# Moving a sort's transposes between matmul steps, and reordering the seven products of one Strassen job

## Chip, cores and metric

The kernel runs on one core of a Trainium2 chip. The metric is the device time of one execution in microseconds. The whole network is one launch; all arithmetic is float32 (a few indices are int32).

Engine names in the profile: PE is TensorE's matmuls and PEld its weight loads, DVE is VectorE, ACT is ScalarE, POOL is GpSimd, SP is SyncE, which only issues DMAs here.

## What is computed

An image of 1024 channels by 64 x 64 pixels goes through four residual layers, each after a group norm:

```python
x = x + _L0_conv_ref(_gn(x), ...)   # per-pixel decay scan over the channels
x = x + _L1_conv_ref(_gn(x), ...)   # 1x1 convolution, 1024 -> 1024
x = x + _L2_conv_ref(_gn(x), ...)   # in_proj, conv, scan in permuted order, gate, out_proj
x = x + _L3_conv_ref(_gn(x), ...)   # 1x1 convolution
```

In layer 2 the pieces that matter here are:

```python
xz = silu(in_proj_w @ x + in_proj_b)
x_ssm, res, gate = split(xz, 3)
xf = silu(conv1d(x_ssm, dw_w) + dw_b)          # three taps along the tokens
perm = _mobius_perm(mobius, H, W)              # per head: argsort of 4096 scores
dbc = dbc_w @ xf + dbc_b                       # dt, B, C of the scan
y = scan(gather(xf, perm), gather(dbc, perm))  # then scattered back
y = y * silu(gate) + res
x = x + silu(out_proj_w @ y + out_proj_b)
```

## The kernel before

The image is kept as 8 blocks of 512 tokens (`FB`), and two blocks make a pair, so there are four pairs (`NP`). All large matrix products use the Strassen-Winograd form: seven products P1 to P7 of half-sized blocks replace eight, at the price of sums on the other engines. With A the weights and B the activations, the outputs are C11 = P1 + P2, C12 = P1 + P6 + P5 + P3, C21 = P1 + P6 + P7 + P4 and C22 = P1 + P6 + P7 + P5 (signs are in the operands).

**The stage with the sort.** The argsort is a bitonic sort of both heads' 4096 scores, written as a generator, `sort_work` (L287). Its `compare` (L295) is eleven small VectorE instructions. For the last five of its twelve rounds the keys have to be transposed and transposed back, which `turn_over` (L324) does: two TensorE transposes into a PSUM bank from `ps_tp`, then a ScalarE copy out of it. The pool behind `ps_tp` has two banks under the tag "tp". The generator yields a word ahead of each piece of work, "compare" or "turn", and `sort_on(quiet, n)` (L373) runs the generator on by at most n compares and returns at each "turn". The sort is a background job: the loops over the matmul steps call `sort_on` once a step with an allowance of compares. Rounds up to 9 are done in layer 1's loop (L915). The rest is done in the loop of L1117, which computes the x_ssm part of in_proj: 56 steps of one product each, 14 a pair, two halves a step. `run(..., fine=True, tell=True)` (L829) yields True in the middle of a product, False after it, and None once the fills of the next pair's operands are issued.

In the same loop the finished tokens go through the convolution and are turned into rows: `follow` (L1040) takes the sums that are ready through `conv`, two steps later into `due3`, and `turn` (L989) does eight matmuls (named l2pt) through two "tp" banks for each of two 128-channel pieces, copies them out on ScalarE to l2xt, adds a part of them on GpSimd, and stores the rest to `tok_d`. The first piece of `due3` is turned in the middle of a step, the other in `follow`.

When the sort is done, its order is stored to `perm_d` and read back as gather indices `src` and scatter indices `dst_` (L361 to L369), all DMAs on GpSimd's queue. The scan stage after it gathers rows by `src`.

On VectorE, TensorE, GpSimd and ScalarE the order of issue in these stages is the program's (`manual_schedule`).

**The two-level jobs.** The gate and out_proj products and layer 3 run in `two_steps` (L1303), with Strassen-Winograd on two levels, 49 products a job, one job a pair and matrix. A job's time is counted in slots, one product each; `plan` (L1376) writes the work of the other engines into a table by slot, `at`. Outer product s of a job has its inner products P1, P2, P6, P7 in slots 7s, 7s+2, 7s+4, 7s+6 and P5, P4, P3 in slots 7s+8, 7s+10, 7s+12, interleaved with the next outer product. Each inner product reads a sum of B's blocks, made by `inner_sum` on GpSimd (four a step), and `emit` (L1492) adds each result into five SBUF tiles: Z (P1, then P6), D (P3), C (P2 + Z), V (P7 + Z, then P4) and Q (P5). At the end C is C11, D is C12, V is C21, Q is C22. For an out_proj job the outer order is `ORDER_B`, P1, P3, P2, P6, P7, P5, P4. `add_in` (L1413) makes the sums between tiles: Z += Q, Q += V, D += Z, a quarter at a time.

The last out_proj job is `final`: its tiles go at once through Silu (ScalarE), the residual sum and `bn_stats` (VectorE) in the slots of the table `done`. After its last statistic comes the group norm of layer 3 (`norm3`, L1552), which the next `two_steps` waits for.

Of the kernel before, what the change touches and what calls it, by code (L numbers as in the profile page):

```python
# [13 lines left out]
ALU = mybir.AluOpType  # L14
# [39 lines left out]
         "P4": (2, "t4"), "P3": (6, "b22")}  # L54
ORDER_A = ["P1", "P2", "P6", "P7", "P5", "P4", "P3"]
ORDER_B = ["P1", "P3", "P2", "P6", "P7", "P5", "P4"]


HN = N // 2
# [29 lines left out]
def tile_net(ctx: ExitStack, tc: tile.TileContext, x, par_d, cst_d, w_d, w2_d, dbcw_d, out):  # L89
    nc = tc.nc  # L90
# [196 lines left out]
    def sort_work():  # L287

        eng, bits = nc.vector, 7
        flip = cst[: HEADS * NT, CST["flip"]]

        def compare(t, new, bit):  # L295
            def two(x):
                v = x.rearrange("p (u s l) -> p u s l", s=2, l=2 ** bit)
                return v[:, :, 0], v[:, :, 1]

            rows, _, w = t.shape  # L300
            a, b = two(t.rearrange("p c w -> p (c w)"))
            (ka, kb), (ia, ib) = two(t[:, 0]), two(t[:, 1])
            (ka2, kb2), (ia2, ib2) = two(new[:, 0]), two(new[:, 1])
            over = swap[0][:rows, :, : w // 2]
            same = swap[1][:rows, 0, : w // 2]
            step = swap[1][:rows, 1, : w // 2]
            def like(x):
                return x.rearrange("p (u l) -> p u l", l=2 ** bit)
            for i, (x, y) in enumerate(((ka, kb), (ia, ib))):
                eng.tensor_tensor(like(over[:, i]), x, y, ALU.is_gt)  # L310
            eng.tensor_tensor(like(same), ka, kb, ALU.is_equal)
            eng.tensor_tensor(same, same, over[:, 1], ALU.mult)
            eng.tensor_tensor(ka2, ka, kb, ALU.min)
            eng.tensor_tensor(same, same, over[:, 0], ALU.add)
            eng.tensor_tensor(like(step), ib, ia, ALU.subtract)
            eng.tensor_tensor(kb2, ka, kb, ALU.max)
            eng.tensor_tensor(step, step, same, ALU.mult)
            eng.tensor_tensor(ia2, ia, like(step), ALU.add)
            eng.tensor_tensor(ib2, ib, like(step), ALU.subtract)

        def negate(v):
            eng.tensor_scalar(v, v, -1.0, None, ALU.mult)

        def turn_over(t, new):  # L324
            rows, _, w = t.shape
            yield "turn"
            pt = ps_tp("sort")
            for c in range(2):
                nc.tensor.transpose(pt[:w, c * rows : (c + 1) * rows], t[:, c], ident[:rows, :rows])
            yield "turn"  # L330
            nc.scalar.copy(new.rearrange("p c w -> p (c w)"), pt[:w, : 2 * rows])  # L331

        now, other = lines
        negate(now.rearrange("p c (u s l) -> p (c u) s l", s=2, l=2)[:, :, 1])
        for k in range(1, 13):
            if k > bits:
                t, t2 = turned_
                yield from turn_over(now, t)
                for bit in reversed(range(k - bits)):
                    yield "compare"  # L340
                    compare(t, t2, bit)
                    t, t2 = t2, t
                yield from turn_over(t, now)
            for bit in reversed(range(min(k, bits))):
                yield "compare"
                compare(now, other, bit)
                now, other = other, now
            if k + 1 < bits:
                v = now.rearrange("p c (u t s l) -> p (c u) t s l", t=2, s=2, l=2 ** k)
                negate(v[:, :, 0, 1])  # L350
                negate(v[:, :, 1, 0])
            elif k + 1 == bits:
                v = now.rearrange("p c (s l) -> p c s l", s=2)
                for s in range(2):
                    eng.tensor_scalar(v[:, :, s], v[:, :, s], flip[:, s : s + 1], None, ALU.mult)
            elif k < 12:
                i = k - bits + 2
                eng.tensor_scalar(now, now, flip[:, i : i + 1], None, ALU.mult)
        eng.tensor_copy(order_i, now[:, 1])
        yield "turn"  # L360
        nc.gpsimd.dma_start(perm_d.rearrange("(a p) o -> a (p o)", p=P), order_i)  # L361
        yield "turn"
        for h in range(HEADS):
            r0, full = h * LC + S, (NK - 1) * LT
            perm = perm_d[h * N : (h + 1) * N]
            for idx in (src, dst_):
                nc.gpsimd.dma_start(idx[r0 : r0 + LT, : NK - 1],
                                  perm[:full].rearrange("(k r) o -> r (k o)", r=LT))
                nc.gpsimd.dma_start(idx[r0 : r0 + N - full, NK - 1 :], perm[full:])  # L369

    coming = [None]

    def sort_on(quiet, n):  # L373


        while coming[0] is not None:
            was = coming[0]
            if was == "compare":
                if n == 0 or not quiet:
                    return  # L380
                n -= 1
            coming[0] = next(order, None)
            if "turn" in (was, coming[0]):
                return


# [566 lines left out]
    with tc.tile_pool(name="l2a", bufs=2) as pa, tc.tile_pool(name="l2a2", bufs=1) as pa2, \  # L953
# [158 lines left out]
        with tc.manual_schedule(engines={E_.DVE, E_.PE, E_.Pool, E_.Activation}):  # L1112
# [4 lines left out]
            for half in run(EARLY + LATE, [WX], normed(norm2), put2a, add2a, before2,  # L1117
                            last_eng=nc.vector, fine=True, tell=True):
                if half:
                    if due3:  # L1120
                        turn(*due3.pop(0))
                elif half is False:
                    follow()
                if half is not None:
                    continue
                i += 1
                if i > 14 and i % 14 == 4:
                    ends = finish(i // 14 - 1)
                next(ends, None)
                sort_on(True, (0, 0, 0, 1, 3, 1, 0, 2, 0, 2, 3, 3, 0, 0)[i % 14])  # L1130
            while coming[0] is not None:
                sort_on(True, 1)

# [158 lines left out]

    wq = ctx.enter_context(tc.tile_pool(name="wq", bufs=10, reuse_waits="tile"))
    xq = ctx.enter_context(tc.tile_pool(name="xq", bufs=4, reuse_waits="tile"))
    bq = ctx.enter_context(tc.tile_pool(name="bq", bufs=13, reuse_waits="tile"))
# [4 lines left out]

    def two_steps(jobs, norm, src_d):  # L1303

        at = {}
        held = {}
        inner = {}
# [68 lines left out]
        def plan(j):  # L1376
            kind, m, pair = jobs[j]
            s0 = j * JOB
            final = j == len(jobs) - 1
            order = ORDER_B if kind == "out" else ORDER_A  # L1380

            def on(slot, f, *a):
                then(s0 + slot, lambda: f(*a))
# [11 lines left out]
            else:  # L1395
                late = [(14, "t1", "b12", "b11"), (15, "t2", "b22", "t1"), (19, "t3", "t2", "b11"), (34, "t4", "b21", "t2")]
                ks = [(2, 3, 0, 1), (2, 3, 0, 1), range(KH), range(KH)]
                put_in = {1: 4, 3: 19}
            for (slot, to, a, b), kk in zip(late, ks):
                for i, k in enumerate(kk):  # L1400
                    on(slot + i, comb, j, to, a, b, k)

            def alias(to, old):
                held[j, to] = tile_of(j, old)
            at[s0 + late[0][0]].insert(0, lambda: alias("t1", "b12"))
            at[s0 + late[2][0]].insert(0, lambda: alias("t3", "b11"))
            at[s0 + late[3][0]].insert(0, lambda: alias("t4", "t2"))
            for s, p in enumerate(order):
                for i in range(4):
                    on(put_in.get(s, 7 * s - 5) + i, inner_sum, j, SIDES[p][1], i)  # L1410
# [4 lines left out]
                eng.tensor_tensor(x, x, y, ALU.add)  # L1415

            q0 = 7 * order.index("P5")
            for row, col, slot, both in ((0, 0, 3, False), (1, 1, 8, False), (1, 0, 10, True), (0, 1, 12, False)):
                on(q0 + slot, add_in, nc.vector if both else nc.gpsimd, "Z", "Q", row, col)
                on(q0 + slot + (0 if both else 1), add_in, nc.vector, "Q", "V", row, col)  # L1420
                if kind == "out":
                    on(q0 + slot + (1 if both else 2), add_in, nc.gpsimd, "D", "Z", row, col)
# [21 lines left out]
                        ("V", 1, 0, {2: 48, 3: 49, 0: 50, 1: 52}), ("Z", 0, 1, {2: 53, 3: 54, 0: 55, 1: 56}))  # L1444
            elif final:
                done = (("C", 0, 0, {0: 27, 1: 28, 2: 29, 3: 30}), ("Q", 1, 1, {2: 46, 3: 47, 0: 49, 1: 50}),
                        ("D", 0, 1, {2: 47, 3: 48, 0: 50, 1: 51}), ("V", 1, 0, {2: 53, 3: 54, 0: 55, 1: 56}))
            else:
                done = (("C", 0, 0, {0: 27, 1: 29, 2: 31, 3: 33}), ("Q", 1, 1, {2: 47, 3: 49, 0: 51, 1: 53}),
                        ("D", 0, 1, {2: 48, 3: 50, 0: 52, 1: 54}), ("V", 1, 0, {2: 55, 3: 57, 0: 59, 1: 61}))  # L1450
# [41 lines left out]
        def emit(j, outer, kind, row, col, ps):  # L1492
# [13 lines left out]
            else:  # L1506
                to = piece(tile_of(j, {"P2": "C", "P6": "Z", "P7": "V", "P4": "V", "P3": "Z"}[outer]), row, col)
                nc.vector.tensor_tensor(to, ps, to, ALU.add)

        def product(j, outer, name):  # L1510

# [26 lines left out]
        for slot in range(min(at), max(max(at), end + 6) + 1):  # L1538
# [2 lines left out]
                step -= 1  # L1541
            if 0 <= step < 7 * len(jobs):
                j, s = divmod(step, 7)
                outer = (ORDER_B if jobs[j][0] == "out" else ORDER_A)[s]
                product(j, outer, ("P1", "P5", "P2", "P4", "P6", "P3", "P7")[i])
            for f in at.get(slot, ()):
                f()
# [109 lines left out]
```

## Time and profile before

| what | us |
|---|---|
| median of 3 runs | 2805.54 (2800.74 to 2807.96) |
| the profiled execution, its own time | 2804.76 |
| its span, first to last instruction | 2802.9 |
| stage with in_proj's x_ssm part and the sort's last three rounds | 623 to 1130 |
| scan stage, with in_proj's res part beside it | 1130 to 1710 |
| gate and out_proj jobs | 1710 to 2446 |
| last out_proj job's slot 42, first product of its P4 | 2412.57 |
| layer 3 | 2446 to 2803 |

The mean granted TensorE clock of the profiled execution is 0.976 of full speed. In the stage with the sort TensorE is busy 474.7 of 507 us, VectorE 251.1, ScalarE 263.7, GpSimd 82.5, and the 16 DMA engines have a mean busy share of 0.41.

How to read the lines below: a timeline line has the start in us, the busy us, the engine, the line of the kernel, the operation, the output and inputs by the program's names, the tile sizes and the number of instructions merged; a bracket says how long the engine stood idle before it, and what ended that. A waits line says who waited for whom: total us, times, longest us.

### The profile page before, as it was taken

The page shows a single profiled execution, that of the slowest core. Times are in us where ns is not written, and L with a number is a line of the kernel's source. Part 1 is how long each engine was busy: PE and PEld are TensorE (multiplying, and loading weights), DVE is VectorE, ACT ScalarE, POOL GpSimd, SP SyncE. Part 2 cuts the span into 40 slices and gives each one's busy share as a digit, 9 for nine tenths or more (in the row PEclk, how much of TensorE's full clock was granted, in tenths as well). Part 3 has the DMA queues.
Part 4 walks back from the last instruction along what each step waited for, and adds up shares of the span by engine and source line. Part 5 has one row for each costly group of instructions (what it writes and reads, how often), then busy time and mean ns, then how long its engine had stood idle before and what let it go on. Part 6 is the DMA issues. An engine that isn't in the chain of part 4 may idle for free.

```text
span 2802.9 us, 30986 instructions
## 1 busy us (share of the span) xinstructions
PE 2631.1 (94%) x9586; PEld 1733.6 (62%) x9586; DVE 1777.2 (63%) x3770; ACT 1091.3 (39%) x1838; POOL 1290.3 (46%) x1170
## 2 busy tenths in 40 slices
PE   5778999999999899999999999999999999799999
PEld 4564444444445455444444446888888888688887
DVE  6986766455455454465666665567676676768776
ACT  4783110104545454475656654313233232221220
POOL 4154324411212002258786774556566565354544
PEclk9998999999999999999999999999999999899999
DMA  7345467644433254486877885889899898678896
GB/s 279 126 148 184 166 214 253 216 146 170 143 103 97 83 164 105 139 260 190 235 200 224 260 217 167 230 240 298 225 269 285 245 294 232 235 261 299 298 328 212
DMA packets 423578, 591.47 MB, mean 211 GB/s; under 512 B 149973, under 2 KB 211541, under 8 KB 420342
## 3 DMA queue, kind: packets, MB, share of 16 engines
q1 hardware_dynamic: 297110, 362.09, 41.3%
q10 hardware_dynamic: 93568, 140.52, 14.2%
q0 software_dynamic: 32736, 86.88, 12.0%
q8 instruction: 78, 1.28, 0.2%
q14 instruction: 86, 0.70, 0.1%
HBM read 432.02 MB, written 157.36 MB: 210 GB/s over the span
## 4 chain that ended last, share of the span: by engine, by line
PE 50%; DMA 3%; DVE 2%; POOL 2%; issue 1%; ACT 1%; DVEq 0%; POOLq 0%; ACTq 0%
PE mm L790 10%; PE q_P7P L1528 5%; PE q_P5P L1528 5%; PE q_P3P L1528 5%; PE q_P6P L1528 5%; PE q_P4P L1528 5%; PE q_P1P L1528 5%; PE q_P2P L1528 4%; PE pg L1208 2%; PE py L1225 2%; DMA qD<-x_d 1%; POOL s L429 1%; PE pr L1184 1%; DMA y_d<-y,dst 0%; POOL t L748 0%
## 5 line engine op out<-in xcount | busy, mean ns | idle before, releaser
L790 PE MATMUL mm<-t,w 128*128 128x512 f32 x1536 | 685.8, 598 | 0.0
L790 PE MATMUL mm<-b,w 128*128 128x512 f32 x1152 | 524.7, 607 | 4.9 <-ACT b L874 4.8
L790 PEld LDWEIGHTS mm<-t,w 128*128 128x128 f32 x1536 | 288.2, 192 | 329.7 <-issue 323.6
L790 PEld LDWEIGHTS mm<-b,w 128*128 128x128 f32 x1152 | 220.0, 195 | 262.4 <-issue 249.1
L979 DVE SCALAR_TENSOR_TENSOR cvp<-xs,par,cvp 128x512 f32<-128x512 f32 x128 | 95.4, 754 | 99.2 <-ACT cvp L976 96.9
L1500 ACT COPY qQ<-q_P5P 128x512 f32<-128x512 f32 x48 | 28.1, 585 | 334.0 <-PE q_P5P L1528 334.0
L1006 POOL TENSOR_TENSOR acc<-l2xt,acc 128x136 f32<-128x136 f32 x56 | 27.9, 500 | 282.2 <-ACT l2xt L1000 279.1
L429 POOL TENSOR_TENSOR s<-s 128x256 f32<-128x256 f32 (+3 forms) x120 | 128.6, 1078 | 7.8
L1335 ACT ACTIVATE qb<-x_x_b,gn_bias,gn_r_r 128x512 f32<-128x512 f32 x128 | 96.8, 806 | 79.3 <-DVE qQ L1463 36.3
L1234 POOL DMA_INDIRECT y_d<-y,dst x74 | 75.2, 1016 | 113.8 <-ACT y L1230 44.8
L1228 ACT COPY g<-py 8x512 f32<-8x512 f32 x146 | 83.7, 574 | 109.6 <-PE py L1225 105.0
L748 POOL TENSOR_TENSOR t<-b,t 128x512 f32<-128x512 f32 x72 | 94.3, 1337 | 56.4 <-DVE t L748 45.8
L1216 DVE TENSOR_TENSOR E<-E,pg 128x512 f32<-128x512 f32 x74 | 50.7, 686 | 107.6 <-PE pg L1208 104.4
L1030 DVE TENSOR_TENSOR xs<-mm,xs 128x512 f32<-128x512 f32 x64 | 41.7, 683 | 121.6 <-PE mm L790 121.5
L888 DVE SCALAR_TENSOR_TENSOR image<-mm,par,image 128x512 f32<-128x512 f32 x64 | 47.1, 746 | 107.6 <-PE mm L790 107.6
L998 PEld LDWEIGHTS l2pt<-both,cv 128*128 128x128 f32 x512 | 77.6, 191 | 53.5 <-issue 25.7
L1331 POOL TENSOR_TENSOR t_t<-qt 128x512 f32<-128x512 f32 x24 | 30.4, 1268 | 161.6 <-DVE qt L1331 86.7
L998 PE MATMUL l2pt<-both,cv 128*128 128x162 f32 x512 | 85.0, 307 | 20.1 <-ACT turned L331 11.5
L1528 PE MATMUL q_P1P<-t_b,wq_P1P 128*128 128x256 f32 x384 | 94.6, 392 | 6.3 <-issue 6.3
L1331 POOL TENSOR_TENSOR t_t<-qt,t_t 128x512 f32<-128x512 f32 x48 | 73.1, 1522 | 52.9 <-DVE qt L1331 52.6
L1528 PE MATMUL q_P4P<-t_t,wq_P4P 128*128 128x256 f32 x384 | 90.6, 379 | 2.2 <-POOL qD L1415 2.2
L1415 DVE TENSOR_TENSOR qQ<-qQ,qV 128x512 f32<-128x512 f32 x48 | 70.9, 1477 | 33.9 <-POOL qZ L1415 33.5
(371 smaller groups left out, 5953.0 us busy)
## 6 DMA issues: line engine op xcount, KB each, us to landing
w<-s_d SPq DMA_DIRECT2D x96, 512.0 KB
w<-in_w_dram SPq DMA_DIRECT2D x72, 512.0 KB
x_x_b<-x_d ACTq DMA_DIRECT2D x32, 1024.0 KB
image<-x_d SPq DMA_DIRECT2D x12, 2048.0 KB
wq_P6P<-s_d SPq DMA_DIRECT2D x84, 256.0 KB
wq_P7P<-s_d SPq DMA_DIRECT2D x84, 256.0 KB
wq_P5P<-s_d SPq DMA_DIRECT2D x84, 256.0 KB
wq_P3P<-s_d SPq DMA_DIRECT2D x84, 256.0 KB
```

Of the source, the lines that this page charges most:

```text
L429: eng.tensor_tensor(out, a, b, ALU.subtract)
L748: eng.tensor_tensor(B[name][k], B[one][k], B[two][k], ALU.subtract)
L790: nc.tensor.matmul(to[o], w[:, k, o * P : (o + 1) * P], B[name][k], start=(fresh and k == 0), stop=(k == KH - 1), skip_group_check=True)
L979: nc.vector.scalar_tensor_tensor(cv, xo[:, at + t : at + t + FB], pcol("dww", 3 * o + t), cv, ALU.mult, ALU.add)
L998: nc.tensor.matmul(pt[:, q * NV : (q + 1) * NV], cv[:, (q0 + q) * P : (q0 + q + 1) * P], both[:, o, :], start=True, stop=True)
L1208: nc.tensor.matmul(pg, bts, cd.rearrange("p s t -> p (s t)"), start=True, stop=True)
L1228: nc.scalar.copy(rows[k + 1][h * LC : h * LC + S, :DH], py[h * LC : h * LC + S])
L1234: nc.gpsimd.indirect_dma_start(out=y_d[:, :], out_offset=bass.IndirectOffsetOnAxis(ap=dst_[:, k : k + 1], axis=0), in_=y[:, :], in_offset= ...
L1331: eng.tensor_tensor(to, a, b, ALU.subtract)
L1335: nc.scalar.activation(tile_of(j, name)[:, k], held[j, "x", name][:, k], AF.Identity, bias=norm[1][:, ct : ct + 1], scale=norm[0][:, ct : ...
L1415: eng.tensor_tensor(x, x, y, ALU.add)
L1528: nc.tensor.matmul(ps[:, o, :], w[:, k, o * P : (o + 1) * P], rhs[:, k, :], start=(new and o == 0 and k == 0), stop=(k == 1), skip_group_c ...
```

## The change

It has two independent parts.

The first concerns the sort in the loop of L1117. The generator now says "turn" only ahead of the transposes, and "take" ahead of the copy out of the bank and of the two groups of index DMAs. `sort_on` returns around anything that isn't a compare. In the middle of a step, a "take" that is due is run before the tokens' turn. After a step, `sort_on` is left out if a transposition is due and `follow` turned tokens in this step (`turned`). The number of instructions stays the same.

The second concerns the last out_proj job alone. Its outer order becomes `ORDER_C`, P1, P3, P2, P5, P6, P7, P4, with P5 two places earlier. The sums between tiles change with it: D += Q first, after P6 D += Z and Q += Z, all on GpSimd; and P7's results are added from PSUM into V and into Q. Tile t4 is made two slots earlier, and in the place of b22. D's Silu, residual sum and statistics come in slots 41 to 44.

```diff
+ORDER_C = ["P1", "P3", "P2", "P5", "P6", "P7", "P4"]
...
                 nc.tensor.transpose(pt[:w, c * rows : (c + 1) * rows], t[:, c], ident[:rows, :rows])
-            yield "turn"
+            yield "take"
             nc.scalar.copy(new.rearrange("p c w -> p (c w)"), pt[:w, : 2 * rows])
...
-        yield "turn"
+        yield "take"
         nc.gpsimd.dma_start(perm_d.rearrange("(a p) o -> a (p o)", p=P), order_i)
-        yield "turn"
+        yield "take"
         for h in range(HEADS):
...
-            if "turn" in (was, coming[0]):
+            if was != "compare" or coming[0] != "compare":
                 return
...
                 if half:
+                    if coming[0] == "take":
+                        sort_on(True, 0)
                     if due3:
                         turn(*due3.pop(0))
                 elif half is False:
+                    turned = bool(due3)
                     follow()
...
-                sort_on(True, (0, 0, 0, 1, 3, 1, 0, 2, 0, 2, 3, 3, 0, 0)[i % 14])
+                if coming[0] != "turn" or not turned:
+                    sort_on(True, (0, 0, 0, 1, 3, 1, 0, 2, 0, 2, 3, 3, 0, 0)[i % 14])
...
+        orders = [ORDER_A if kind != "out" else ORDER_B if j + 1 < len(jobs) else ORDER_C
+                  for j, (kind, _, _) in enumerate(jobs)]
...
-            order = ORDER_B if kind == "out" else ORDER_A
+            order = orders[j]
...
+            if order is ORDER_C:
+                late[3] = (32, *late[3][1:])
...
-            at[s0 + late[3][0]].insert(0, lambda: alias("t4", "t2"))
+            at[s0 + late[3][0]].insert(0, lambda: alias("t4", "b22" if order is ORDER_C else "t2"))
...
             q0 = 7 * order.index("P5")
-            for row, col, slot, both in ((0, 0, 3, False), (1, 1, 8, False), (1, 0, 10, True), (0, 1, 12, False)):
+            for row, col, slot in ((0, 0, 3), (1, 1, 9), (1, 0, 11), (0, 1, 13)) if order is ORDER_C else ():
+                on(q0 + slot, add_in, nc.gpsimd, "D", "Q", row, col)
+                for to in "DQ":
+                    on(q0 + 7 + slot, add_in, nc.gpsimd, to, "Z", row, col)
+            for row, col, slot, both in ((0, 0, 3, False), (1, 1, 8, False), (1, 0, 10, True),
+                                         (0, 1, 12, False)) if order is not ORDER_C else ():
...
             elif final:
                 done = (("C", 0, 0, {0: 27, 1: 28, 2: 29, 3: 30}), ("Q", 1, 1, {2: 46, 3: 47, 0: 49, 1: 50}),
-                        ("D", 0, 1, {2: 47, 3: 48, 0: 50, 1: 51}), ("V", 1, 0, {2: 53, 3: 54, 0: 55, 1: 56}))
+                        ("D", 0, 1, {2: 41, 3: 42, 0: 43, 1: 44}), ("V", 1, 0, {2: 53, 3: 54, 0: 55, 1: 56}))
...
+                nc.vector.tensor_tensor(to, ps, to, ALU.add)
+            if outer == "P7" and orders[j] is ORDER_C:
+                to = piece(tile_of(j, "Q"), row, col)
                 nc.vector.tensor_tensor(to, ps, to, ALU.add)
...
-                outer = (ORDER_B if jobs[j][0] == "out" else ORDER_A)[s]
+                outer = orders[j][s]
                 product(j, outer, ("P1", "P5", "P2", "P4", "P6", "P3", "P7")[i])
```

## The prediction

> **What bounds the kernel now.** I read the page's busy shares first, then TensorE's waits stretch by stretch, then the timeline where the two edited places run, last the chain that ended last. The page says who carries the time:
>
> ```profile
> PE 2631.1 (94%) x9586; PEld 1733.6 (62%) x9586; DVE 1777.2 (63%) x3770; ACT 1091.3 (39%) x1838; POOL 1290.3 (46%) x1170
> ```
>
> TensorE is busy in 94% of the span, so an edit is worth what it takes out of TensorE's idle time. The stage with the sort and the tokens' turns is the loop of L1117 (623 to 1130 us). TensorE's waits between 650 and 1012 us are only these:
>
> ```profile
> PE l2pt L998 <- ACT turned L331: 11.5, 3, 3.8
> PE sort L329 <- ACT l2xt L1000: 8.6, 3, 3.4
> PE l2pt L998 <- ACT l2xt L1000: 3.4, 6, 0.6
> ```
>
> The columns are total us, times, longest. All three belong to the sort: its transposes wait for one of the two "tp" banks, then hold one while the tokens' turns (l2pt) need both. TensorE's timeline around the second of three such places:
>
> ```profile
> 815.86 3.60 PE L790 MATMUL mm<-b,w 128*128 128x512 f32 x8
> 819.29 1.26 PE L998 MATMUL l2pt<-both,cv 128*128 128x162 f32 x8
> 823.95 0.47 PE L329 MATMUL sort<-cst,lines 64*128 64x64 f32 x2 [3.39 <-ACT l2xt L1000]
> 824.35 5.13 PE L790 MATMUL mm<-b,w 128*128 128x512 f32 x8
> 829.32 0.71 PE L998 MATMUL l2pt<-both,cv 128*128 128x162 f32 x4
> 830.59 0.82 PE L998 MATMUL l2pt<-both,cv 128*128 128x162 f32 x4 [0.56 <-ACT l2xt L1000]
> 840.04 0.71 PE L998 MATMUL l2pt<-both,cv 128*128 128x162 f32 x4
> 844.59 1.45 PE L998 MATMUL l2pt<-both,cv 128*128 128x162 f32 x4 [3.84 <-ACT turned L331]
> 845.84 4.55 PE L790 MATMUL mm<-t,w 128*128 128x512 f32 x8
> ```
>
> See a 3.39 us wait, eight matmuls in 5.13 us instead of 3.60, turns cut in two, and a 3.84 us wait, again with slow matmuls behind it. ScalarE shows why the last is long:
>
> ```profile
> 841.48 2.91 ACT L874 ACTIVATE b<-image,gn_bias,gn_r_r 128x512 f32<-128x512 f32 x4
> 844.30 0.24 ACT L331 COPY turned<-sort 128x128 f32<-128x128 f32 x1
> ```
>
> The copy that frees the bank takes 0.24 us but is queued behind 2.91 us of fills for the next pair. The end of the last out_proj job:
>
> ```profile
> 2430.52 1.89 PE L1528 MATMUL q_P4P<-qt,wq_P4P 128*128 128x256 f32 x8
> 2436.93 0.67 DVE L1508 TENSOR_TENSOR qV<-q_P4P,qV 128x512 f32<-128x512 f32 x1
> 2444.29 1.97 DVE L178 BATCH_NORM_AGGREGATE gn_mv<-stats 128x2 f32<-128x48 f32 x8
> 2446.31 0.59 PE L192 MATMUL gn_pg<-gn_mv,cst 128*128 128x8 f32 x2 [13.90 <-DVE gn_mv L178]
> ```
>
> TensorE ends at 2432.4 and waits 13.90 us, because VectorE is still clearing Q, D and V; the chain of waits runs through VectorE from 2419.7 on.
>
> **What the Trainium skill says.** "TensorE: Matmul & The Clock Gate", section "What's actually happening": an idle window of about 3.4 us halves the clock, and as much work restores it. This trace agrees roughly: after 3.38 to 3.84 us idle, eight matmuls take 4.4 to 6.4 us for 3.43. "PSUM — Partial Sum Buffer", section "Engine vs sequencer instructions": ScalarE, VectorE and GpSimd queues are strict FIFO; the copy behind the fills shows it. "SBUF — State Buffer", section "SBUF: two separate sides": a VectorE operation with two SBUF inputs and a GpSimd operation exclude each other on a shared port; here GpSimd's 128x512 subtraction takes 1.27 us, and 1.72 us beside VectorE's qQ<-qQ,qV at 2411.
>
> **Part 1, the sort.** Removed: the three pairs of waits. I take start-to-start times in TensorE's timeline against the undisturbed rhythm (4 turn matmul groups 1.10 us, 8 matmuls 3.43, two sort transposes 0.26). At the first place (695 to 723 us) the excess is 1.95 + 0.11 + 0.83 + 0.83 + 4.20 + 1.61 = 9.5 us; at the second (819 to 850) 3.70 + 1.54 + 0.83 + 0.83 + 4.70 + 0.95 = 12.6; at the third (946 to 979) 3.69 + 3.01 + 0.83 + 0.83 + 4.11 + 1.70 = 14.2. Together 36.2 us, of which 23.5 are the waits above and the rest restarts and a slow clock.
>
> Where does the sort go? Turns come four steps after the sums that feed them, so follow() turns tokens in the steps with i mod 7 = 1 to 4, and 5, 6 and 0 are free. Walking the generator with the loop's allowances (they stay; only when a transposition may go changes): before, the transpositions come in steps 8, 11, 22, 26, 36 and 40; after, in 12, 19, 26, 33, 40 and 48, each copied out in the first half of the next step, where no turn is due. Free banks, so neither they nor the turns wait: the three waits are gone. The transposes are the same ten pairs; those before step 0 don't move, since that loop has no half steps and "take" returns as "turn" did.
>
> What is late next: in steps 8 to 10 the turns need ScalarE's copies in time. Steps 50 to 52 of before show these without a transposition: the excess there is 0.93 + 0.11 + 0.42 + 0.11 = 1.6 us. For three places 4.7 us (bounds 0 and 8). In step 10 the fills stay ahead of the turns' own copies: a turn's copy ends some 8.7 us after the step starts (fills end at +7.8, from 717.3 - 709.5), and the next turn wants the bank at 3.43 + 1.10 + 3.43 = 8.0; about 0.5 us each, 1.5 in all (bounds 0 and 5). Compares move with it: steps 9, 23, 37, 51 get two, 10, 24, 38, 52 up to three, of 11 instructions that take 1.99 us (lines, at 1073.5) or 1.43 (turned, at 844.6); VectorE's next sums are due at step 12, so the rhythm of 9 us a step covers these 10 us; uncovered they would delay sums by at most 4 us each time (taken: 0). The perm_d DMA on GpSimd moves from the end of step 50 to the middle of 53, its loads from 51 to 53: 16.7 us of issuing on GpSimd's queue (1080.7 to 1097.5), with only the token sums (L1006) behind it, three xt buffers deep and no turns after step 53 until 1124. The first gather is at 1165.8, some 60 us after step 53, so the later sort costs nothing; without that slack it costs its 2.5 steps, some 20 us. Part 1: 36.2 - 4.7 - 1.5 = 30 us (bounds 20 and 36).
>
> **Part 2, the last out_proj job.** One product takes 1.73 us, a slot. Before, VectorE has 39 operations from slot 42 (2412.6): 8 for P4, 3 for P5, 4 sums, 24 for Q, D and V. After: 8 for P4, 8 for P7 (V and Q, in slots 43 to 47), 22 for D, Q and V, together 38; D's first two and most of P7's lie ahead in slots 35 to 41, where VectorE has room. So the load is nearly the same and the gain lies in idle time and port conflicts: 39 operations took 2414.5 to 2444.3, 0.76 each; undisturbed (2428.5 to 2444.3) 23 took 15.8, 0.69 with the wait for P4, some 0.66 without. If VectorE starts at 2414.5 and takes 0.62 each: 38 x 0.62 = 23.6, end at 2438.1, a gain of 6.2: the upper bound.
>
> Against it: GpSimd gets 12 sums in place of 7. In slots 30 to 34 five sums and four inner sums, in 37 to 41 six and four. At 1.24 us each (2408.60 to 2409.82 to 2411.05) the first nine end near slot 37, with a microsecond for t4's four subtractions on VectorE; the next ten near 44.5 to 45. P7's last sum into Q's upper right piece (slot 43, VectorE there at 45.2 in my walk) waits for the tenth: just in time. Behind it on VectorE stand P4's reads, for which TensorE's banks wait (slots 46 to 54), and D's last two. Walking VectorE's queue with 0.66 us an operation from there ends at slot 58.6, 2441.2: a gain of 3 us. With 1.5 us per GpSimd sum the tenth ends at 46.6, and the gain is 0.7; with two more such holds it is -2. Taken: 3 (bounds -2 and +6). ScalarE loses nothing: P5's puts merely come earlier. Weight DMAs on SP keep their number; D's fetch and store on ScalarE's queue come some 6 slots earlier, and nothing waits for them. The norm and the next step's start keep their length.
>
> **Sum.** 30 + 3 = 33 us. The profiled execution took 2804.76 (span 2802.9 and 1.9 around it); 2804.76 - 33 = 2771.8. The median of the runs is 0.8 above it, so 2772.5, given as 2772.
>
> **Rivals.**
> - ScalarE takes over: with the banks free, turns wait for ScalarE's copies in steps 8 to 11 of each pair, to twice both bounds above (2 x 8 = 16 us), and Part 2 gives nothing: 2805.5 - 20 = 2785. For it: the 0.93 us in step 51; against it: ScalarE is busy 264 of 507 us in the stage.
> - The job's end loses: GpSimd's sums hold VectorE, -2 us, the sort gains 30: 2777. For it: 19 GpSimd operations in 12 slots; against it: 1.24 us each.
> - No change: the stage is held by something the waits hide, such as weights; 2805. Against it: no DMA is among TensorE's waits there, and the DMA share is 0.41.
> - Slower: the sort does not finish in its stage. If a pair offered one window instead of two, 14 line compares and 5 turned ones would be left, 14 x 1.99 + 5 x 1.43 = 35 us, and two transpositions, 2 us, which L1131 puts on VectorE ahead of everything, with TensorE idle: -33 + 37 = +4, 2809. It decides when over 33 us, about 17 compares, are left after step 55; my walk leaves none, the last falls in step 52.
>
> **How the numbers follow.** Forecast 0.60, the job's end losing 0.19, ScalarE 0.13, no change 0.04, slower 0.04. Faster by over 0.3% (8.4 us, about what a measurement of this kernel can tell from none) 0.92, within 0.04, slower 0.04. The range: 30 to 36 with +6 gives 2763; 20 with -2 gives 2787; it holds the first three cases for the most part.
>
> **What would show it.** In the stage no wait of l2pt on turned or lines, none of sort on l2xt, transposes outside the turns, the clock full; the stage some 30 us shorter. At the job's end gn_mv starts about 3 us sooner after slot 42, and VectorE's first hold, if any, is at Q's P7 sum behind GpSimd. I am wrong if l2pt's waits on l2xt sum to over 10 us, or if the gathers wait for src.

## The result

The changed kernel takes 2771.98 us, the median of four runs (2765.41 to 2775.17), against 2806.75 for four runs of the kernel before on the same chip (2800.74 to 2807.97). The ratio is 0.9872, with a 95% interval from 0.9856 to 0.9888: 1.3% faster, as forecast (2772). Its profiled execution took 2769.34 us, with a span of 2767.6.

Lines of the kernel are counted in the new file here: the sort's transposes are at L330 and their copy at L332, the turns' matmuls at L999 and their copy at L1001, the products at L1547, and the new add of P7 into Q at L1527. In runs that add lines the same statements stand a few lines further down.

First the page of the kernel after: busy us, share of the span and number of instructions, by engine.

```profile
PE 2617.4 (95%) x9586; PEld 1728.1 (62%) x9586; DVE 1771.5 (64%) x3773; ACT 1089.5 (39%) x1838; POOL 1300.5 (47%) x1175
```

TensorE has the same 9586 matmuls and is still the engine that sets the time; 13.7 us of its busy time are gone as well, 13.4 of them in the stage with the sort, where matmuls behind a long wait had run slowly. VectorE has three instructions more, GpSimd five more: the last job's sums.

To see where the rest went, cut both spans at the same events. "Stage" is from the first matmul of in_proj's x_ssm part to the first turn after its last product; "scan" from the first gather to the start of the last eight matmuls of in_proj's res part; "gate" stands for the two-level jobs behind it; slot 42 is the first product of P4 in the last out_proj job; gn_mv is the start of the norm's aggregation behind that job.

| stretch, us | before | after | difference |
|---|---|---|---|
| start to first matmul of the stage | 627.6 | 625.7 | -1.9 |
| stage | 497.2 | 461.6 | -35.6 |
| last turns to first gather | 41.0 | 41.5 | +0.5 |
| scan | 538.7 | 542.3 | +3.6 |
| end of scan, gate to slot 42 | 708.0 | 709.2 | +1.2 |
| slot 42 to gn_mv | 31.7 | 30.1 | -1.6 |
| gn_mv to the end | 358.6 | 357.1 | -1.5 |

Two of the rows are the change: the stage with the sort (30 forecast) and the job's end (3 forecast). The others have not been touched and scatter: over all runs below, the scan row lies between 538.3 and 544.1 us, the jobs' row between 706.6 and 711.8 and the last one between 356.9 and 359.8. Kernels that are the same up to the scan's end differ by as much as before and after do: 538.3 us in the last run below, with the stage and scan of after, against its 542.3. The two edited rows hardly scatter: five kernels with the new stage and nothing added to it have 461.6 to 462.4 us, and six with the new job end have 30.10 to 30.20.

The waits of TensorE from 640 to 1060 us in the kernel after (total us, times, longest) are now one line, in place of the three lines of 11.5, 8.6 and 3.4 us that the prediction shows.

```profile
PE sort L330 <- DVE swap L318: 1.2, 1, 1.2
```

This wait is new. It is the sort's last transposition, which now comes right behind the compare that makes its keys; it stands at the same place in every run with the new steps:

```profile
1023.03 0.66 PE L330 MATMUL sort<-cst,turned 128*64 128x128 f32 x2 [1.21 <-DVE swap L318]
```

How a transposition passes now, in TensorE's timeline of after (start, busy, what, number merged):

```profile
837.61 5.31 PE L791 MATMUL mm<-t,w 128*128 128x512 f32 x12
842.85 0.33 PE L330 MATMUL sort<-cst,lines 64*128 64x64 f32 x2
843.12 7.13 PE L791 MATMUL mm<-t,w 128*128 128x512 f32 x16
```

and ScalarE's timeline at the same place:

```profile
845.54 2.92 ACT L875 ACTIVATE t<-image,gn_bias,gn_r_r 128x512 f32<-128x512 f32 x4
848.36 0.24 ACT L332 COPY turned<-sort 128x128 f32<-128x128 f32 x1
```

Three things are to be seen. The transposes take 0.27 us from start to start and leave no gap on either side. The copy out is still behind 2.92 us of fills, and comes more than 5 us after its transposes. And that costs nothing now, because no turn asks for a bank in this step: matmuls run through at 0.43 us each. The wait was not shortened, it was put where nobody stands behind it.

At the job's end, VectorE's timeline of after, around the place that the prediction names as its first possible hold:

```profile
2384.78 1.67 DVE L1483 TENSOR_TENSOR qD<-qD,x_x_D 128x512 f32<-128x512 f32 x1
...
2387.09 0.67 DVE L1521 TENSOR_TENSOR qV<-q_P7P,qZ 128x512 f32<-128x512 f32 x1
2387.68 0.68 DVE L1527 TENSOR_TENSOR qQ<-q_P7P,qQ 128x512 f32<-128x512 f32 x1
...
2410.42 1.74 DVE L179 BATCH_NORM_AGGREGATE gn_mv<-stats 128x2 f32<-128x48 f32 x7
```

and GpSimd's last two sums in the same run:

```profile
2384.64 1.26 POOL L1426 TENSOR_TENSOR qD<-qD,qZ 128x512 f32<-128x512 f32 x1
2385.86 1.72 POOL L1426 TENSOR_TENSOR qQ<-qQ,qZ 128x512 f32<-128x512 f32 x1
```

GpSimd's last sum ends at 2387.58, and P7's add into Q starts on VectorE at 2387.68. From 2387.09 to gn_mv at 2410.42 VectorE has 35 operations in 23.3 us, 0.67 each, and stands idle for 1 us in all. TensorE now even waits for VectorE's reads before its last products (2.1 us for qV at 2394.6; of 2.8 us more at 2399.4 the trace doesn't show the cause). Its own end moves from 19.8 to 24.5 us after slot 42, and its wait for gn_mv shrinks from 13.9 to 7.7 us. That fall of 6.2 us is mostly a wait that has moved to an earlier place; the norm starts only 1.6 us sooner.

### The profile page after: what moved, and what is told of

The parts are those of the page before. It is cut to its first block, busy times and chain, and to the rows that moved or that the text cites. A ratio compares the mean times of both kernels' runs of the same rounds, so it can differ in the third digit from the quotient of the medians.

```text
span 2767.6 us, 30985 instructions
## 1 busy us (share of the span) xinstructions
PE 2617.4 (95%) x9586; PEld 1728.1 (62%) x9586; DVE 1771.5 (64%) x3773; ACT 1089.5 (39%) x1838; POOL 1300.5 (47%) x1175
## 3 DMA queue, kind: packets, MB, share of 16 engines
q8 instruction: 78, 1.28, 0.2%
## 4 chain that ended last, share of the span: by engine, by line
PE 49%; POOL 3%; DMA 3%; DVE 3%; issue 1%; ACT 1%; SPq 0%; DVEq 0%; POOLq 0%; ACTq 0%
PE mm L791 9%; PE q_P5P L1547 5%; PE q_P3P L1547 5%; PE q_P7P L1547 5%; PE q_P6P L1547 5%; PE q_P4P L1547 5%; PE q_P1P L1547 5%; PE q_P2P L1547 4%; PE pg L1213 2%; PE py L1230 2%; DMA qD<-x_d 1%; POOL s L430 1%; POOL t L749 1%; PE pr L1189 1%; DMA g<-tok_d,src 0%
## 5 line engine op out<-in xcount | busy, mean ns | idle before, releaser
L791 PE MATMUL mm<-b,w 128*128 128x512 f32 x1152 | 516.9, 600 | 5.4 <-ACT b L875 4.8
L999 PEld LDWEIGHTS l2pt<-both,cv 128*128 128x128 f32 x512 | 77.0, 191 | 35.6 <-issue 25.6
L1547 PE MATMUL q_P1P<-t_b,wq_P1P 128*128 128x256 f32 x384 | 92.2, 385 | 6.6 <-issue 6.6
L1547 PE MATMUL q_P4P<-t_t,wq_P4P 128*128 128x256 f32 x384 | 91.5, 381 | 4.9 <-issue 2.8
L1547 PE MATMUL q_P2P<-t_b,wq_P2P 128*128 128x256 f32 x384 | 92.2, 384 | 0.0
L875 ACT ACTIVATE b<-image,gnl_bias,gnl_r_r 128x512 f32<-128x512 f32 x48 | 36.8, 808 | 137.4 <-DMA s<-in_w_dram 58.5
```

What stands on the lines that cost most here:

```text
L791: nc.tensor.matmul(to[o], w[:, k, o * P : (o + 1) * P], B[name][k], start=(fresh and k == 0), stop=(k == KH - 1), skip_group_check=True)
L999: nc.tensor.matmul(pt[:, q * NV : (q + 1) * NV], cv[:, (q0 + q) * P : (q0 + q + 1) * P], both[:, o, :], start=True, stop=True)
L1547: nc.tensor.matmul(ps[:, o, :], w[:, k, o * P : (o + 1) * P], rhs[:, k, :], start=(new and o == 0 and k == 0), stop=(k == 1), skip_group_c ...
```

## The experiments

**The two parts by themselves.** The first kernel keeps the sort's edits and puts the last job back:

```diff
-        orders = [ORDER_A if kind != "out" else ORDER_B if j + 1 < len(jobs) else ORDER_C
+        orders = [ORDER_A if kind != "out" else ORDER_B if j + 1 < len(jobs) else ORDER_B
...
-                        ("D", 0, 1, {2: 41, 3: 42, 0: 43, 1: 44}), ("V", 1, 0, {2: 53, 3: 54, 0: 55, 1: 56}))
+                        ("D", 0, 1, {2: 47, 3: 48, 0: 50, 1: 51}), ("V", 1, 0, {2: 53, 3: 54, 0: 55, 1: 56}))
```

> The changed kernel with its second part undone (the last out_proj job in the order and sums of before). Theory (the sort's hold of a bank cost the stage 36 us, and nothing took its place): the stage from its first matmul to the first turn of the tail (627.6 to 1124.9 before, 497.2 us) takes 461 to 463 us, as in the changed kernel; slot 42 to the norm's aggregate takes 31.7 us as before; time 2771 to 2776 us, ratio 0.988 to 0.990. Rival (the two parts share the gain, the job's end gives 5 us or more of it): time 2777 us or more. The scan stage from its first gather to its last matmul took 538.7 us before and 542.3 in the changed kernel: if the later sort or the shifted start causes the difference it is near 542 here too, if it is scatter of single executions it may be anything from 537 to 544.

Measured: 2767.75 us (2764.22 to 2768.52), ratio 0.9855 [0.9833, 0.9876], a little less than expected; stage 462.3 us, slot 42 to gn_mv 31.70, both as expected. The second keeps the job and undoes the sort's edits in the loop:

```diff
                 if half:
-                    if coming[0] == "take":
-                        sort_on(True, 0)
                     if due3:
...
-                if coming[0] != "turn" or not turned:
-                    sort_on(True, (0, 0, 0, 1, 3, 1, 0, 2, 0, 2, 3, 3, 0, 0)[i % 14])
+                sort_on(True, (0, 0, 0, 1, 3, 1, 0, 2, 0, 2, 3, 3, 0, 0)[i % 14])
```

> The changed kernel with its first part undone (the sort as before), the last out_proj job in the new order. Theory (VectorE stays the bound at the job's end, a little less is in its queue): the sort's stage takes 497 us as before, slot 42 to the norm's aggregate 30.1 us in place of 31.7, TensorE's wait for the aggregate 7 to 8 us in place of 13.9; time 1 to 3 us below before, ratio 0.999 to 1.000. Rival (the new order is worth the 5 us that single profiles leave over beside the sort): 2801 us or less.

Measured: 2805.18 us against 2805.08, ratio 0.9999 [0.9991, 1.0007]; stage 496.9, slot 42 to gn_mv 30.11, and TensorE's three lines of waits as in before. So the sort's part is the whole gain, within what can be measured. The job's 1.6 us is there at its place, the same in each run, but the 1 to 3 us that were expected of it don't show in the total: the interval reaches from a gain of 2.5 us to a loss of 2.0.

**The two halves of the sort's part.** The change does two things: it lets transposes go only in steps without turns, and it copies them out half a step after they went, where the program had a whole step before. That is an earlier copy: in before, ScalarE's copy out starts 18.8, 20.4 and 21.8 us after the transposes at the three places that cost, in after 5.5 to 7.0 us. First only the earlier copy (the condition on `turned` removed, as in the last lines of the diff above); "half a step later" in the expectation is counted from the transposes:

> The changed kernel with one line of the first part undone: transposes may go in any step again, the copy out of the bank stays half a step later. They go to steps 8, 11, 22, 25, 36, 39, all with turns. Theory (two causes: a transposition right behind four groups of turns waits for their copies, 8.6 us with slow matmuls behind it, 14 us in all; a bank held over the next turns costs the rest): only the second goes, the stage takes 497 - 36 + 14 + 3 = 478 us, sort waits on l2xt for 8 to 9 us in three places, no wait on turned over 1 us; time about 2788. Rival (the late copy behind the fills is all that cost): stage 462, time 2772. Second rival (in turned steps the copy still comes too late): stage over 488.

Measured: 2782.22 us, ratio 0.9905 [0.9885, 0.9926]; stage 476.8. At those three places the copy starts 4.6 us after the transposes. TensorE's waits from 640 to 1060 us:

```profile
PE sort L330 <- ACT l2xt L1001: 8.5, 3, 3.4
PE l2pt L999 <- ACT l2xt L1001: 0.5, 1, 0.5
PE l2pt L999 <- ACT turned L332: 0.4, 1, 0.4
```

The waits of the turns for a bank that the sort holds are gone but for 0.4 us; the transposes' own wait for a bank that the turns hold (8.5 us, as in before) is left, with what follows it. In TensorE's timeline of this run:

```profile
817.36 0.47 PE L330 MATMUL sort<-cst,lines 64*128 64x64 f32 x2 [3.37 <-ACT l2xt L1001]
817.77 6.61 PE L791 MATMUL mm<-b,w 128*128 128x512 f32 x8
```

Eight matmuls take 6.61 us for 3.60. Then only the free steps (the first two lines of that diff removed, the condition kept):

> The changed kernel with the other line of the first part undone: transposes only in steps without turns, the copy out at the step's end as before. The steps are 12, 19, 26, 33, 40, 48 as in the changed kernel, the copies come half a step later, in steps where no turn is due before the next one; the sort ends one and a half steps later (perm_d in step 54). Theory (free steps alone remove every wait, the half step is worth nothing to the time): stage 461 to 463 us, time 2769 to 2775, within 0.2% of the changed kernel, no wait of a gather for its indices. Rival (the half step carries part of the gain): stage 466 or more, with waits of l2pt on turned or lines.

Measured: 2770.72 us, ratio 0.9865 [0.9844, 0.9886]; stage 463.8, just above the expected 461 to 463 and below the rival's 466. The copies start 12.5 to 15.1 us after the transposes, and yet there is a single wait in that stretch beside the 1.2 us that after has too:

```profile
PE l2pt L999 <- ACT lines L332: 1.4, 1, 1.4
```

So of the stage's 35.6 us the free steps alone bring 33.4, and the earlier copy alone 20.4. The halves overlap: each takes away nearly all of the turns' wait for the sort's bank, and only the free steps take away the sort's wait for the turns' banks. Beside the free steps the earlier copy is worth a single wait of 1.4 us, and 1.4 to 2.2 us of the stage, which has 461.6 to 462.4 us with both.

**What new waits the sort could have brought.** The prediction took 4.7 us for new waits of the turns in steps 8 to 10, read from steps 50 to 52 of before, which run without a transposition. In after the turns of these steps have none of that. Here are the start of the turn in step 50 of before, VectorE's sums at that time, and the next turn with its wait:

```profile
1074.42 1.26 PE L998 MATMUL l2pt<-both,cv 128*128 128x162 f32 x8
1077.47 1.27 DVE L1030 TENSOR_TENSOR xs<-mm,xs 128x512 f32<-128x512 f32 x2
1079.88 1.37 PE L998 MATMUL l2pt<-both,cv 128*128 128x162 f32 x8 [0.77 <-ACT l2xt L1000]
```

and the same turn and sums in step 22 of after:

```profile
807.30 1.26 PE L999 MATMUL l2pt<-both,cv 128*128 128x162 f32 x8
807.56 1.27 DVE L1031 TENSOR_TENSOR xs<-mm,xs 128x512 f32<-128x512 f32 x2
```

In before, the compares, the last block's extra operations and the cast of `order_i` pushed the sums to 3.05 us after the start of the turn; in after they start 0.26 us after it, and the next turn follows at 811.84 without a wait. The only excess of the turns in after is 0.3 us at each of three places, 0.9 in all, and it is of the other kind that the prediction priced, at 1.5 us: the turn at 825.62 follows its bank's copy at 825.16, which stood behind 2.92 us of fills. To try whether the late sums cause the waits of before, the changed kernel got five adds of a scratch tile, 128x512, on VectorE. No result uses them.

> The changed kernel with five more 128x512 adds of a scratch tile on VectorE in steps 9, 23, 37 and 51, ahead of the sums of the next block (about 3 us a step; no result uses them). Theory (in before's steps 50 to 52 the turns waited because VectorE's sums came some 3 us later there than in ordinary steps, so those steps overstated what the new kernel would wait): the turn after each such step waits 0.7 to 1.6 us for ScalarE's copy l2xt, which without the adds it does not, and the stage grows by 4 to 6.5 us. Rival (those waits in before came from the half steps or the fills, not from late sums): no wait of l2pt on l2xt in these steps and the stage within 1 us of the changed kernel's 461.6.

Measured: 2777.18 us, but not for that reason: the stage has 462.5 us, without a wait of l2pt. The adds came where VectorE has nothing due (at 718 us it stood idle for 14 us right after them), and the tile's clearing, issued ahead of the stage, held VectorE for 13.4 us, until a DMA (`s_d`) of an earlier stage was done; TensorE then waited 7.4 us for the image's adds, and the stage began at 636.2 instead of 625.7. The run tells only that 3.6 us on VectorE after step 9 are covered. Moved to where the sums are due:

```diff
+        junk = pa.tile([P, FB], F32, name="junk", bufs=1)
...
+                if i == 2:
+                    nc.vector.memset(junk, 0.0)
+                if i % 14 == 7:
+                    for _ in range(5):
+                        nc.vector.tensor_tensor(junk, junk, junk, ALU.add)
             while coming[0] is not None:
```

> As the run before with five extra VectorE adds, but these now stand at the end of steps 7, 21, 35 and 49, directly ahead of the sums of steps 8, 22, 36 and 50 (in the run before they stood after step 9, where the next sums are not due for some 14 us), and the scratch tile is cleared inside the stage. Theory (the turns in steps 50 to 52 of before waited because VectorE's sums came some 3 us later there than in ordinary steps): sums some 3.3 us later, so the turn half a step later waits 1.2 to 1.8 us for l2xt, and the one after it some tenths; over three or four places the stage grows by 4 to 9 us over 461.6 and the time with it. Rival (those waits came from the half steps or the fills): no wait of l2pt on l2xt there, stage within 1 us of 461.6.

Measured: 2778.49 us, ratio 0.9902 [0.9882, 0.9922]; stage 474.1. VectorE's timeline of this run, then TensorE's:

```profile
814.79 3.58 DVE L1141 TENSOR_TENSOR junk<-junk 128x512 f32<-128x512 f32 x5
818.29 1.28 DVE L1032 TENSOR_TENSOR xs<-mm,xs 128x512 f32<-128x512 f32 x2
```

```profile
814.52 1.26 PE L1000 MATMUL l2pt<-both,cv 128*128 128x162 f32 x8
...
820.70 1.37 PE L1000 MATMUL l2pt<-both,cv 128*128 128x162 f32 x8 [1.48 <-ACT l2xt L1002]
...
825.77 1.37 PE L1000 MATMUL l2pt<-both,cv 128*128 128x162 f32 x8 [0.26 <-ACT l2xt L1002]
```

The sums start 3.8 us after the turn, and the pair of waits that before shows in steps 50 and 51 (0.77 and 0.26 us) appears at three places, its first wait alone at the fourth: seven waits, 7.7 us. That late sums make such waits is shown. The stage's growth, 12.5 us, is more than the 4 to 9 expected; beside the waits, matmuls at the fourth place slowed down by 1.7 us (last section), and the stage's first 48 matmuls, ahead of any of these adds, took 23.6 us for 22.6, because the clock stayed at half for 5.6 us of the stage in place of 3.4.

**What bounds the job's end.** Two theories stood open for the job's small gain: the length of VectorE's row, or the order. In the next run six of VectorE's residual adds (all of Q, two of D) went to GpSimd, which is idle from 2387.6 on, and their statistics two slots later:

```diff
+                    spare = orders[j] is ORDER_C and (name == "Q" or (name == "D" and k < 2))
...
-                            nc.vector.tensor_tensor(c, c, held[j, "x", name][:, k], ALU.add)
-                            quarter_stats(tile_of(j, name), row, nb, k)
+                            eng = nc.gpsimd if spare else nc.vector
+                            eng.tensor_tensor(c, c, held[j, "x", name][:, k], ALU.add)
+                            if not spare:
+                                quarter_stats(tile_of(j, name), row, nb, k)
                     on(slot, one)
+                    if spare:
+                        on(slot + 2, lambda name=name, row=row, nb=nb, k=k: quarter_stats(tile_of(j, name), row, nb, k))
```

> The changed kernel, with the residual adds of Q (all four) and of D's first two pieces in the last out_proj job on GpSimd instead of VectorE, their bn_stats two slots later: six operations leave VectorE's queue. Theory (VectorE's row of operations is what ends the job): gn_mv starts 25.5 to 26 us after slot 42 instead of 30.1, TensorE's wait for it falls or stays near 5 to 8 us because its own end comes earlier too, and the time falls by 4 to 5 us, to about 2767. Rival (GpSimd's adds come too late behind its sums, or share the port with VectorE so that its operations stretch): gn_mv 29.5 us or more after slot 42, no gain.

Measured: slot 42 to gn_mv 24.87 us instead of 30.11 (25.5 to 26 expected), a gain of 5.2 where the job's whole change brought 1.6; time 2764.68 us (2759.4 to 2768.57), ratio 0.9851 [0.983, 0.9872]. TensorE's wait for gn_mv is 8.5 us, a little above the range, as its own end came earlier by 6.1. The same with the old order of products, and all eight adds of Q and D on GpSimd:

> The sort's part of the change alone with the old order of the last out_proj job (P7 before P5), and the residual adds of Q and D (all eight) of that job on GpSimd, their bn_stats two slots later. Theory (how many operations VectorE has to clear after slot 42 sets the job's end, and the order of products does not): gn_mv 25.5 to 27 us after slot 42 instead of 31.7, the time some 5 us under the sort's part alone, about 2762 to 2764. Rival (GpSimd's own sums, which in the old order last until about slot 51, hold the adds): gn_mv 30 us or more after slot 42, no gain.

Measured: 2768.34 us, ratio 0.9866 [0.9845, 0.9887]; 30.44 us to gn_mv against 31.70 with the adds on VectorE. My theory that only the number of operations counts is wrong; the rival holds. In GpSimd's timeline of this run

```profile
2398.19 1.26 POOL L1426 TENSOR_TENSOR qD<-qD,qZ 128x512 f32<-128x512 f32 x1
...
2401.86 2.55 POOL L1486 TENSOR_TENSOR qD<-qD,x_x_D 128x512 f32<-128x512 f32 x2
```

the sums of the old order last until 2399.4, 18 us after slot 42 (2381.05); some of the adds stand between them and the last four behind them, until 2404.4; VectorE's statistics wait for them, with V's operations behind. So the new order has a worth that its own run does not show: its sums on GpSimd end 7.3 us after slot 42, early enough to take work from VectorE. The two runs differ in the number of adds as well, eight against six; six adds in the old order were not run, so how much of the 5.2 us it would keep is open.

Once more, the version with six adds on GpSimd, and the changed kernel beside it on the same chip:

> The changed kernel with six residual adds on GpSimd once more, on the same chip as the next run, to tell whether it beats the changed kernel. Theory: 4 to 5.5 us less than the changed kernel. Rival: what the job gains is lost in the scatter of the stages between, difference under 2 us.

> The changed kernel itself once more, for comparison on the same chip: about 2770.

Measured: 2764.49 us (2763.28 to 2766.43) and 2769.07 us (2764.22 to 2774.51), with 24.87 and 30.13 us to gn_mv. With the earlier runs there are nine of each: medians 2764.7 and 2769.3, 4.7 us apart, which fits the 5.2 seen at the place. By the medians the version with six adds is the fastest of the kernels tried, at a ratio to before of 0.9851 [0.9829, 0.9874] in this set; the two intervals against before overlap, so the difference rests on the medians and on the place.

**What held VectorE at Q's P7 add.** D's four residual adds were put five slots later:

```diff
-                        ("D", 0, 1, {2: 41, 3: 42, 0: 43, 1: 44}), ("V", 1, 0, {2: 53, 3: 54, 0: 55, 1: 56}))
+                        ("D", 0, 1, {2: 46, 3: 47, 0: 48, 1: 49}), ("V", 1, 0, {2: 53, 3: 54, 0: 55, 1: 56}))
```

> The changed kernel with D's four residual adds in the last out_proj job five slots later (slots 46 to 49 in place of 41 to 44), so that none of them runs beside GpSimd's last sums. Theory A (the two adds that GpSimd's sums stretched to 0.99 and 1.67 us are what made the job's gain 1.6 us instead of 3): gn_mv 28.6 to 29 us after slot 42, against 30.11. Theory B (the stretched adds only filled time in which VectorE would have waited for GpSimd's last sum into Q anyway): VectorE stands idle about 1.5 us ahead of Q's P7 add and has four more operations behind it, gn_mv 31 to 32 us after slot 42.

Measured, from one execution (2771.47 us): 31.77 us to gn_mv. Theory B holds. VectorE's timeline of this run has this wait:

```profile
2385.39 0.69 DVE L1527 TENSOR_TENSOR qQ<-q_P7P,qQ 128x512 f32<-128x512 f32 x1 [2.05 <-POOL qQ L1426]
```

Without D's adds beside them GpSimd's last two sums take 1.28 us each, and the last ends at 2385.36, 6.4 us after slot 42 in place of 7.3. But VectorE stands idle for 2.05 us ahead of it, and D's operations are still to come.

## Why the prediction was right

**Part 1.** The step "the three waits are gone, and the sort goes into free steps" held, but for one wait that the walk did not have: the last transposition waits 1.2 us for its compare, 1.6 us of excess. The sum can be checked. Removed are the 36.2 us of the three places and also the 1.6 us of steps 50 to 52, which the prediction left standing; new are 0.9 of the turns and the 1.6 of that transposition. That gives 35.3 us, and the stage fell by 35.6. That the slow matmuls behind the waits go too, beyond the 23.5 us of waits themselves, was right and was a third of the gain. Mis-sized was the term for new waits of the turns: of 4.7 us nothing came, and of 1.5 us behind the fills 0.9. The step that failed is taking steps 50 to 52 as the picture of steps 8 to 10: there VectorE was late by work that belongs to the last block and the sort's end, and steps 8 to 10 have none of it. The run with the late sums shows that this lateness makes just such waits. The walk of steps, allowances and GpSimd's queue was right as well: perm_d is issued at 1062.7 (step 53's turns start at 1061.0), its eight loads from 1068.0 to 1078.0, and the first gather comes at 1128.8; so some 50 us of slack cover the later sort.

**Part 2.** "Just in time" was right, though both came a slot later than in the walk: VectorE reached Q's P7 add at slot 46.3 (45.2 in the walk), 0.1 us after GpSimd's tenth sum had ended. From there VectorE took 0.67 us an operation, where 0.66 was taken. The size was off, 1.6 us for 3. The mis-sized term is the end of that tenth sum: taken at slot 44.5 to 45, it was 2387.58, 7.27 us or 4.2 slots after slot 42, thus slot 46.2. GpSimd's ten operations from 2373.60 on took 1.40 us each, not 1.24; the prediction's other walk, with 1.5 us a sum and an end at 46.6, gives 0.7, and the measured gain lies between the two. A part of it is D's two adds, which run beside GpSimd's sums and stretch to 0.99 and 1.67 us; the last run shows that without them the sum would end at slot 45.7, still late, and that moving them makes the job's end later.

**Rivals.** ScalarE does not take over: turns wait for its copies 0.9 us in these steps, not 8 or 16. The rival of the job's end was right on the place and wrong on the sign. The sort finishes as walked: its order is stored in the middle of step 53.

**Sum.** 35.6 + 1.6 = 37.2 us at the two places, against 33 forecast; other rows gave back 1.8 on balance, most of all the scan, so that the profiled execution fell by 35.4 us. The medians are 34.8 apart. That the forecast met the median to a microsecond is luck in part: Part 1 was low by 5.6, Part 2 high by 1.4, and the rest lies in rows that no edit touched.

## What to carry to other kernels

A background job that shares two buffers with the main job is best placed where the main job doesn't use them: the copy that frees the bank may then come 5.5 us after the transposes at no cost, or 12.5 to 15.1 us at the cost of one wait of 1.4 us, while a copy 3.2 to 4.6 us after them in the wrong steps still leaves 15.2 of the 35.6 us. When TensorE's waits are priced, the restarts and slow matmuls behind them belong to the price: here 23.5 us of waits stood for 36.2 us of excess. And a stretch taken as a picture of another must have the same work on the engines ahead of it in the chain; a look at when VectorE's sums start in both would have shown that steps 50 to 52 were no picture of steps 8 to 10.

## What the runs showed that I had not expected

How short a wait can slow TensorE down depends on where it falls. In the run with late sums, eight matmuls after waits of 1.86, 1.48 and 1.49 us took 3.60 us as always, but at the fourth place

```profile
1057.05 1.68 PE L1000 MATMUL l2pt<-both,cv 128*128 128x162 f32 x8 [2.05 <-ACT l2xt L1002]
1058.52 5.02 PE L791 MATMUL mm<-b,w 128*128 128x512 f32 x8
```

after 2.05 us they took 5.02. "TensorE: Matmul & The Clock Gate", section "What's actually happening" of the Trainium skill says that the clock halves after an idle window of about 3.4 us, and that this window runs free of what the kernel does. The clock records of the traces agree on the grid: in all thirteen, the granted clock is either full or half, and it changes only on a fixed grid of 3.41 us. They differ on the idle time: a window need not be idle throughout. Here the clock was half from 1057.97 to 1061.39 us, and the window before it, from 1054.56, held the whole wait, 2.05 of its 3.41 us. The waits of 1.48 and 1.49 us also lay in one window each, and that of 1.86 us was cut by an edge at 702.99 into 1.21 and 0.65 us; none of them halved the clock. In after, 2.08 us ahead of P4's products (2394.64) were cut at 2393.83, with no more than 1.42 us of idle time in either window, and left the clock full. Over all thirteen traces from 240 us on, no window at full clock with less than 1.49 us between TensorE's matmuls was followed by half clock, and every one with more than 1.98 us was; in between both occur. So whether a wait of 2 us costs 1.7 us more, as here, or next to nothing is a chance of where the grid cuts it.

The price of VectorE's and GpSimd's shared port is seen from both sides: D's residual add took 1.67 us beside GpSimd's sums and 0.68 elsewhere, GpSimd's sum 1.72 and 1.27. The trace agrees with what the prediction cites on it: the add that starts at 2384.78 ends at 2386.45, just 0.55 us after GpSimd's sum does (2385.90), and GpSimd's next sum ends 1.13 us after this add. That fits with each waiting in turn for the other to end: both paid.
